# One more item for the last items' expert, and results finished in groups of four tiles

## The chip, the cores and the metric

One core of a Trainium2 chip runs one program. TensorE (PE) multiplies, VectorE (DVE) and ScalarE (ACT) work element by element, GpSimd (POOL) here issues indirect DMAs and computes powers, SyncE (SP) issues most of the other DMAs. The metric is the device time of one execution in microseconds (us).

## The reference

Two layers over 2048 tokens (2 sequences of 1024) of 512 numbers, all in float32. The first is a gated recurrence with a residual; the second a mixture of eight experts of which each token uses two.

```python
x = x + layernorm(minGRU(layernorm(x)))          # 512 -> 2*768 -> scan over 1024 -> 512
y = layernorm(x)
w, e = top_k(y @ gate_kernel, 2); w = softmax(w) # two experts of each token
out = sum over c of w[c] * (silu(y @ w0[e_c]) * (y @ w1[e_c])) @ wo[e_c]
x = x + layernorm(out)
```

An expert has two matrices of 512 x 1024 (w0, w1) and one of 1024 x 512 (wo), 2 MB each, 6 MB together.

## The kernel before, in words

**Blocks and tiles.** The 2048 tokens are four blocks of 512 tokens, a block is four tiles of 128. The recurrence goes block by block. As soon as a block's tokens are through it, they are routed: each of a token's two choices gets a row in a scratch list of its expert (`xs`), in the order of arrival, and POOL scatters the tokens there.

**Items.** The experts' work is cut into items: a run of up to 512 tokens of one expert. An item's tokens are read back from `xs` (four DMAs on SP, `fetch_tokens`), transposed by VectorE (`turn_in`), and multiplied in `run`: for each of 8 pieces of the hidden dimension, 4 matmuls with w0 and 4 with w1, silu on ScalarE, the product on VectorE, and 4 matmuls with wo. The columns of these matmuls are the item's tokens, rounded up to 8. The number of columns is known only at run time, so TensorE's program holds a copy (an arm) of the item for every size, and jumps to the right one (`Switch` in `emit`); `announce` hints at the next one. The result is transposed into `yo` and stored to `ys` by four DMAs, 256 KB each, issued when the next item's first matmul starts (`refill` calls `store`, `fetch_weights` for the next item, and `fetch_tokens` for a later one).

**Which items there are.** The first item runs while the last block is still being routed; it takes up to 512 tokens of the expert that has most in the first three blocks (`first_table`). The rest is planned from the counts on VectorE in `other_tables`. The expert with most tokens in the fourth block becomes the *last items' expert*: its tokens of tiles 12 to 14 are kept back for an item of their own (`last[0]`, slot `S_Z1` of `ys`), and tile 15 is computed for that expert as a dense tile straight from `late_y` (`last[1]`, `run_dense`). Everything else goes into `NR` = 14 regular items: every expert gets as many as its tokens need at 512 each, and the items that are left over are given one by one to the expert with most tokens per item (`most(length)`). An expert's tokens are spread evenly over its items, with sizes rounded up to 8. Regular items run in the order of experts. Weights lie in two buffers; an item's weights are loaded while the one before runs. The last item and the dense tile share one set.

**Finishing.** `places` works out for every token and choice in which row of `ys` its result stands. For each tile, two gathers (indirect DMAs on POOL) fetch the two results; ScalarE scales the first by its weight, VectorE adds the second, takes mean and variance, POOL raises the variance to the power -1/2, VectorE normalises and adds the residual, SP writes the tile out. Tiles 0 to 11 depend on the regular items alone; tiles 12 to 14 also on the last item's store. Tile 15 is gathered early without the last expert's part, and gets the dense tile's product at the very end (`finish_last`). Twelve pairs of buffers `got` hold the gathered rows; they lie on the weight buffer that the last items do not use. Tiles 12 to 15 use those of tiles 0 to 3 again.

**Order.** TensorE's order is the order of the recording. The other engines' orders come from a list scheduler (`schedule`) that simulates the program with the times written beside each operation (`ns`, `load`); `follows` adds an order without a wait, `urgent` puts an operation first. All orders are fixed when the kernel is built; an engine never overtakes within its own queue.

The lines that matter: the gathers come from `gather` (L1112 in the profile), the item's matmuls from `mm` in `run` (L1036), token transposes from `turn_in` (L999), DMAs from `dma` (L499); L303 is the recorder through which every other operation goes, so these are told apart by their tiles.

Of the kernel before, what the change touches and what calls it, by code (L numbers as in the profile page):

```python
# [319 lines left out]
def mingru_then_moe(nc, x, w_hg, w_out, w_gate, w0, w1, wo, out):  # L320
# [30 lines left out]

    B, S, D = x.shape
    DI = w_out.shape[0]
    E = w_gate.shape[1]
# [54 lines left out]
    minus_half, z_no, first_n, last_n, z1_n = (few[:, i : i + 1] for i in range(5))  # L411
    tw_late = few[:, 6:7]
    by = keep("by", [P, 4, E])
    first_e, total, z_one, count, start_e, so_far = (
# [6 lines left out]
    before_half = keep("before_half", [P, E])  # L421
    nums = {}
    for name, shape, pattern, base in (
        ("expert", [P, NT, E], [[0, NT], [1, E]], 0),
# [84 lines left out]


    g.POOL.memset(minus_half, -0.5)
    g.POOL.memset(ones, 1.0)
    g.POOL.affine_select(
        ident, ones, pattern=[[-1, P]], compare_op=ALU.is_equal, fill=0.0, base=0, channel_multiplier=1, ns=300
# [211 lines left out]
    def in_steps(n):  # L726
# [14 lines left out]

    def other_tables():

        pc = turn("tp", tp)[:, 0:E]
        g.PE.matmul(pc, ones, routed[NB - 1][1][:, NT - 1, :], start=True, stop=True, ns=280)
        g.DVE.tensor_copy(before_half, pc)
        pc = counts()
        g.DVE.tensor_copy(total, pc)
        new = little([P, E])
# [71 lines left out]
        z_row, z_at = little([P, E]), little([P, 1])  # L821
        g.DVE.tensor_add(z_row, before_half, first_row)
        g.DVE.tensor_mul(z_row, z_row, z_one)
        g.DVE.tensor_reduce(z_at, z_row, AX.X, ALU.add)
        g.DVE.tensor_copy(table_z[:, 1:2], z_at)
        g.DVE.tensor_copy(table_z[:, 0:1], z_no)
        z2, z2_n = little([P, E]), little([P, 1])
        g.DVE.tensor_sub(z2, total, before_half)
        g.DVE.tensor_mul(z2, z2, z_one)
        g.DVE.tensor_reduce(z2_n, z2, AX.X, ALU.add)  # L830
        g.DVE.tensor_sub(z1_n, last_n, z2_n)
        g.DVE.tensor_scalar(table_z[:, 3:4], in_steps(z1_n), -1.0, 0.0, ALU.add, ALU.max)

        g.DVE.tensor_scalar(by[:, 3, :], start, 2.0, float(W), ALU.add, ALU.mult)

    def places(c):
# [32 lines left out]
        g.DVE.tensor_scalar(z, z, z1_n, float((S_Z1 + 1) * W), ALU.subtract, ALU.add)  # L869

        late = slice(n - 1, n)
        early = little([P, 1])
# [36 lines left out]
    def fetch_tokens(it, behind=(), follows=()):  # L909

        j = it.no
        z = z_item[j % 2]
        if it is last[1]:
# [87 lines left out]
    def branch(its):  # L1001

        group = cells(its[0], 2)
        if len(its) > 1:
            group = table_i[0:1, 2, :]

        def load(e):
            for it in its:
# [15 lines left out]
    def run(it, gaps=()):  # L1024
# [8 lines left out]
        def mm(dst, w, rhs, first, last):  # L1033
            return g.add(
                "PE",
                lambda e, n: e.matmul(dst[:, W - n : W], w, rhs[:, W - n : W], start=first, stop=last),  # L1036
                [w, rhs] if first else [w, rhs, dst], [dst], 460 if most < W else 862, columns=1,
            )

        def down_part(m, q):  # L1040
# [4 lines left out]
        for m in range(KM):  # L1045
# [15 lines left out]
            if m == KM - 2 and it is not last[0]:  # L1061
                if it is first:
                    branch(regular)
                    branch(last[:1])
                announce(items[j + 1])
        yo = yo_item[j % 2]

# [11 lines left out]

    def run_dense(it):  # L1080

        g.item = last[0]
# [22 lines left out]
        return po[0]  # L1105


    def gather(dst, rows, slots, lane, i, follows=()):
        source = ys[0 : (slots[-1] + 1) * W, :]
        return g.add(  # L1110
            "POOL",
            lambda e: e.indirect_dma_start(dst, None, source, bass.IndirectOffsetOnAxis(ap=rows, axis=0)),  # L1112
            [rows] + [("ys", j, b) for j in slots for b in (*range(NQ), "nought")], [dst], 1450,
            lane=lane, batch=(i, lane), load=P * D * 4 / 320, follows=follows,
        )

    def finish(i):

        y0, y1 = got[0][i % NG], got[1][i % NG]
        for c, dst in ((0, y0), (1, y1)):  # L1120
            if i < TT - NT:
                o = gather(dst, where_i[:, c, i : i + 1], range(NR + 1), f"got{i % NG}", i)
            elif i < TT - 1:
                o = gather(dst, where_i[:, c, i : i + 1], range(S_Z1 + 1), f"got{i % NG}", i)
            else:
                o = gather(dst, where_early[:, c : c + 1], range(S_NONE + 1), f"got{i % NG}", i)
            gathers.append(o)
        g.ACT.activation(y0, y0, AF.Copy, scale=tw[:, 0, i : i + 1])
        g.DVE.scalar_tensor_tensor(y0, y1, tw[:, 1, i : i + 1], y0, ALU.mult, ALU.add)
        y0_v, y1_v, x_v = (  # L1130
            v.rearrange(how, c=NQ, b=NQ)
            for v, how in (
                (y0, "p (b c j) -> p b c j"), (y1, "p (c b j) -> p b c j"), (x_sb[i], "p (c b j) -> p b c j"),
            )
        )
        if i == TT - 1:
            g.DVE.tensor_copy(y1_v, y0_v)
            return y1
        mean, rstd = mean_and_rstd(y0)
        g.DVE.tensor_scalar(y0, y0, mean, rstd, ALU.subtract, ALU.mult)  # L1140
        g.DVE.tensor_add(y1_v, y0_v, x_v)
        dma("SP", of[ts(i, P), :], y1, f"out{i % NG}", P * D * 4, writes=[("out", i)])

    def finish_last(y, term):
        g.DVE.scalar_tensor_tensor(y, term, tw_late, y, ALU.mult, ALU.add)
# [15 lines left out]
    for t in range(NT - 1):  # L1161
# [18 lines left out]
    scan(  # L1180
        3, range(0, KE),
        gaps(
            [(turn_y, 2, 0), (turn_y, 2, 1)], [(rank, 1), (turn_y, 2, 2), (route, 2, 0, in_po)],
            [(turn_y, 2, 3), (route, 2, 1, in_po)], (route, 2, 2, in_po), (route, 2, 3, in_po), (),
            [(rank, 2), (first_table,)],
        ),
# [32 lines left out]
    drain(list(scattered.values()))  # L1219
    for it in items[1:-1]:  # L1220
        if it.no > 1:
            turn_in(items[it.no + 1], *((3, 4) if it is last[0] else ()))
        run(it)
    store(last[0])
    term = run_dense(last[1])
    gathers = []
    for i in (*range(TT - NT), TT - 1, *range(TT - NT, TT - 1)):
        if i == TT - 1:
            y = finish(i)
        else:  # L1230
            finish(i)
    drain(gathers)
    finish_last(y, term)

    g.emit()

# [41 lines left out]
```

## Time and profile before

| | us |
|---|---|
| runs | 998.93, 994.41, 998.54; median 998.54 |
| the profiled execution | 998.32 |
| its span (first to last instruction) | 996.3 |
| TensorE busy | 963.8 (97%) |
| VectorE, ScalarE, POOL busy | 434.8, 151.9, 110.4 |
| first regular item to the last item's end | 372.7 to 956.8 |
| the dense tile and all behind it | 956.8 to 996.3 |

The item sizes are the columns in the rows of L1036: the first item has 512, the regular ones, in the order of time, 256, 256, 256, 232, 232, 216, 136, 280, 288, 224, 216, 264, 264 and 128, the last item 272, the dense tile 128. Every matmul of float32 shows as two rows of TensorE, so an item has 192: 128 with w0 and w1, 64 with wo.

How to read what follows: in a list in order of time, the first two numbers are start and length in us, counted from the span's start; "x" is how many instructions were merged; the bracket is the engine's idle time before it and what ended it, where "issue" means that the profile shows nothing that was waited for. In a table of stretches each engine has its busy time and instruction count, followed by PEclk (the granted clock of TensorE, 1.00 is full speed), the mean busy share of the 16 DMA engines, and the GB/s moved.

### The profile page before, as it was taken

To read this page: it belongs to the slowest core of one execution; us is meant where nothing else is said; L and a number is where in the kernel's file an instruction comes from. 1 tells how busy PE (TensorE), PEld (TensorE's weight loads), DVE (VectorE), ACT (ScalarE), POOL (GpSimd) and SP (SyncE) were. 2 spreads that over 40 slices of the span, in tenths; PEclk is the share of its full clock that TensorE was granted. 3 is DMA by queue.
4 is the path that set the end of the run, shared out by engine and by line. 5 is a ranking of instruction groups with operands and counts; after the bars stand their busy time and mean duration, and the time that the engine had idled before them with its cause. 6 is when DMAs were issued, how large, how long until landed. Compare 5 with 4: busy or idle time off the path is not lost.

```text
span 996.3 us, 10882 instructions
## 1 busy us (share of the span) xinstructions
PE 963.8 (97%) x4086; PEld 713.8 (72%) x4086; DVE 434.8 (44%) x929; ACT 151.9 (15%) x269; POOL 110.4 (11%) x144
## 2 busy tenths in 40 slices
PE   6999999999999999999999999899999999998994
PEld 4444454555445448888899999787799988897882
DVE  6643636565465943313323324313224323142676
ACT  2222020212112001111011011110010110111221
POOL 3200104014312000000000000000000000000673
PEclk9999999999999999999999999999999999999997
DMA  9910002002821369596495696965475883836583
GB/s 298 388 64 1 0 1 86 0 1 95 273 108 64 126 192 320 163 279 231 110 324 171 183 316 190 325 188 208 132 258 159 262 289 66 293 129 214 151 256 130
DMA packets 140856, 175.40 MB, mean 176 GB/s; under 512 B 6112, under 2 KB 77792, under 8 KB 140768
## 3 DMA queue, kind: packets, MB, share of 16 engines
q1 hardware_dynamic: 132368, 155.22, 48.4%
q0 software_dynamic: 5120, 16.78, 5.1%
q10 hardware_dynamic: 3280, 2.10, 0.8%
q8 instruction: 70, 1.15, 0.5%
q14 instruction: 18, 0.15, 0.0%
HBM read 135.02 MB, written 39.06 MB: 175 GB/s over the span
## 4 chain that ended last, share of the span: by engine, by line
PE 91%; DMA 2%; POOL 2%; DVE 2%; issue 1%; ACT 0%; SPq 0%; DVEq 0%
PE bank L1036 63%; PE bank L303 28%; DMA got<-ys_scratch,where_i 2%; POOL got L1112 1%; DVE got L303 1%; POOL little L303 1%; DVE little L303 1%; DMA x<-in_L_attn_x_dram 0%; ACT got L303 0%; DVE inter L303 0%; DVE xn_in L303 0%; ACT xT L303 0%; ACT si L303 0%; SPq L1273 0%; DVEq L257 0%
## 5 line engine op out<-in xcount | busy, mean ns | idle before, releaser
L1036 PE MATMUL bank<-xTi,w 128*128 128x256 f32 (+10 forms) x2048 | 451.7, 379 | 8.0 <-issue 7.9
L1036 PEld LDWEIGHTS bank<-xTi,w 128*128 128x128 f32 x2048 | 369.3, 191 | 76.8 <-issue 37.3
L303 DVE TENSOR_TENSOR inter<-si,bank 128x512 f32<-128x512 f32 (+1 forms) x136 | 90.1, 662 | 371.1 <-PE bank L1036 370.8
L1036 PE MATMUL bank<-inter,wo 128*128 128x256 f32 (+10 forms) x1024 | 228.2, 376 | 0.0
L1036 PEld LDWEIGHTS bank<-inter,wo 128*128 128x128 f32 x1024 | 184.5, 190 | 33.9 <-issue 14.6
L303 PE MATMUL bank<-xT,whg 128*128 128x512 f32 (+1 forms) x400 | 171.5, 580 | 0.2 <-ACT xT L303 0.2
L303 ACT ACTIVATE si<-bank 128x512 f32<-128x512 f32 (+1 forms) x136 | 78.4, 577 | 557.3 <-PE bank L1036 555.7
L303 PEld LDWEIGHTS bank<-xT,whg 128*128 128x128 f32 x400 | 74.3, 192 | 77.5 <-issue 75.5
L1112 POOL DMA_INDIRECT got<-ys_scratch,where_i x30 | 31.1, 1036 | 602.2 <-DMA ys_scratch<-yo 594.7
L303 PE MATMUL bank<-wout,h 128*128 128x512 f32 x192 | 84.2, 595 | 0.0
L303 PEld LDWEIGHTS bank<-wout,h 128*128 128x128 f32 x192 | 35.9, 190 | 43.2 <-issue 41.1
L303 POOL TENSOR_TENSOR little<-little,few 128x1 f32<-128x1 f32 x64 | 40.3, 632 | 229.2 <-DVE little L303 228.9
L999 DVE STREAM_TRANSPOSE xTi<-zi 128x2048 f32<-128x2048 f32 (+2 forms) x18 | 63.3, 3514 | 4.5 <-DMA zi<-xs_scratch 4.5
L303 DVE STREAM_TRANSPOSE yo<-bank 128x512 f32<-128x512 f32 (+1 forms) x64 | 45.0, 702 | 37.1 <-PE bank L1036 33.7
L303 DVE SCALAR_TENSOR_TENSOR s<-bank,s 128x512 f32<-128x512 f32 x24 | 16.6, 690 | 78.8 <-ACT s L303 78.8
L704 POOL DMA_INDIRECT xs_scratch<-y,row_i x32 | 33.5, 1046 | 47.5 <-DVE little L303 33.7
L303 ACT ACTIVATE z<-bank 128x512 f32<-128x512 f32 x24 | 14.3, 597 | 109.5 <-PE bank L303 109.5
L303 DVE BATCH_NORM_STATS2 little<-x 128x6 f32<-128x512 f32 x32 | 21.7, 682 | 8.2 <-DMA x<-in_L_attn_x_dram 7.7
L303 ACT ACTIVATE s<-bank 128x512 f32<-128x512 f32 x24 | 14.3, 597 | 57.0 <-PE bank L303 57.0
L303 PEld LDWEIGHTS bank<-wg,yT 128*128 128x128 f32 x128 | 16.4, 192 | 5.3 <-issue 5.3
L303 PEld LDWEIGHTS bank<-ident,xn_in 128*128 128x128 f32 x64 | 8.6, 155 | 15.7 <-DVE little L303 8.7
L303 PE MATMUL bank<-ident,xn_in 128*128 128x128 f32 x64 | 11.2, 303 | 8.4 <-DVE little L303 8.3
(131 smaller groups left out, 366.7 us busy)
## 6 DMA issues: line engine op xcount, KB each, us to landing
w<-in_L_ffn_w_kernel_dram SPq DMA_DIRECT2D x64, 1024.0 KB, 9.0
wo<-in_L_ffn_wo_kernel_dram SPq DMA_DIRECT2D x32, 1024.0 KB, 14.0
zi<-xs_scratch SPq DMA_DIRECT2D x64, 256.0 KB, 5.5
ys_scratch<-yo SPq DMA_DIRECT2D x58, 256.0 KB, 10.1
xs_scratch<-nought SPq DMA_DIRECT2D x8, 1024.0 KB, 12.6
out_dram<-got SPq DMA_DIRECT2D x15, 256.0 KB, 3.0
x<-in_L_attn_x_dram SPq DMA_DIRECT2D x14, 256.0 KB, 7.8
whg<-in_L_attn_w_hg_dram SPq DMA_DIRECT2D x10, 256.0 KB, 6.7
```

Of the source, the lines that this page charges most:

```text
L303: return program.add(eng, lambda e: getattr(e, name)(*args, **kw), ins, [out], ns, urgent=urgent, follows=follows)
L704: lambda e, c=c, i=i: e.indirect_dma_start(xs, bass.IndirectOffsetOnAxis(ap=row_i[:, c, i : i + 1], axis=0), y_of[i], None),
L999: g.add("DVE", lambda e: e.transpose(dst, src), [z], [dst], 3900 // parts, follows=follows)
L1036: lambda e, n: e.matmul(dst[:, W - n : W], w, rhs[:, W - n : W], start=first, stop=last),
L1112: lambda e: e.indirect_dma_start(dst, None, source, bass.IndirectOffsetOnAxis(ap=rows, axis=0)),
```

## The change

Three things change.

*One more item.* The last items' expert gets an item for its tokens of the third block as well, as far as the first item did not take them (`z0_e`; `count_two` counts the tokens of blocks one and two for it). It has its own slot `S_Z0` in `ys`, can have any size up to 512, and runs between the regular items and the item of tiles 12 to 14. The regular items are planned for what is left; their number `NR` stays. Tiles 0 to 7 now wait for regular items alone, tiles 8 to 11 also for the new item's store.

*Groups.* The tiles are finished in groups of a block: all gathers of a group, then per tile the weighted sum and the statistics, then one power for the group's four variances (three in the last group), then normalising, residual and output tile by tile. A group's power is placed on POOL behind the gathers of the next group, and tile 15's two gathers come before the third group's power.

*Planner's times.* The scheduler's assumed times for gathers, for stores of the last items and for the new item's matmuls are changed.

```diff
-    NI = NR + 3
-    S_NONE, S_Z1 = NR + 1, NR + 2
+    NI = NR + 4
+    S_NONE, S_Z0, S_Z1 = NR + 1, NR + 2, NR + 3
...
+    def count_two():
+        pc = counts()
+        g.DVE.tensor_copy(before_two, pc)
...
+        g.DVE.tensor_max(z0_e, before_two, first_e)
+        g.DVE.tensor_sub(z0_e, so_far, z0_e)
...
-        g.DVE.tensor_scalar(z, one, last_n, None, ALU.mult)
+        g.DVE.scalar_tensor_tensor(z, z0_e, last_n, one, ALU.add, ALU.mult)
...
+        split = (NB - 1) * NT
+        g.DVE.tensor_scalar(z[:, 0:split], z[:, 0:split], z0_n, float((S_Z0 + 1) * W), ALU.subtract, ALU.add)
+        g.DVE.tensor_scalar(z[:, split:], z[:, split:], z0_n, z1_n, ALU.subtract, ALU.subtract)
+        g.DVE.tensor_scalar(z[:, split:], z[:, split:], float((S_Z1 + 1) * W), None, ALU.add)
...
-    last = [Item(NR + 1 + i, S_Z1, sizes[: LATE // STEP], (NR + 1) % 2) for i in range(2)]
+    last = [
+        Item(NR + 1 + i, slot, some, (NR + 1) % 2)
+        for i, (slot, some) in enumerate(((S_Z0, sizes), (S_Z1, sizes[: LATE // STEP]), (None, None)))
+    ]
...
-                load=most * P * 4 / (90 if it.no == NR else 320),
+                load=most * P * 4 / (160 if it.no >= NR else 320),
...
-                [w, rhs] if first else [w, rhs, dst], [dst], 460 if most < W else 862, columns=1,
+                [w, rhs] if first else [w, rhs, dst], [dst], 460 if it.no > NR else 862, columns=1,
...
-            [rows] + [("ys", j, b) for j in slots for b in (*range(NQ), "nought")], [dst], 1450,
-            lane=lane, batch=(i, lane), load=P * D * 4 / 320, follows=follows,
+            [rows] + [("ys", j, b) for j in slots for b in (*range(NQ), "nought")], [dst], 1270,
+            lane=lane, batch=(i, lane), load=1270,
...
+    def terms(i):
+
+        for c in range(2):
+            if i == TT - 1:
+                where, slots = where_early[:, c : c + 1], S_NONE
+            else:
+                where, slots = where_i[:, c, i : i + 1], (NR, NR, S_Z0, S_Z1)[i // NT]
+            o = gather(got[c][i % NG], where, range(slots + 1), f"got{i % NG}", i)
+        return o
...
+    def total_of(i):
         y0, y1 = got[0][i % NG], got[1][i % NG]
         g.ACT.activation(y0, y0, AF.Copy, scale=tw[:, 0, i : i + 1])
         g.DVE.scalar_tensor_tensor(y0, y1, tw[:, 1, i : i + 1], y0, ALU.mult, ALU.add)
...
+    def finish(tiles, behind):
+
+        n = len(tiles)
+        mv, rstd = little([P, n, 2]), little([P, n])
+        sums = [total_of(i) for i in tiles]
+        for k, (y0, _) in enumerate(sums):
+            st = little([P, 6])
+            g.DVE.bn_stats(st, y0)
+            g.DVE.bn_aggr(mv[:, k, :], st)
+        g.DVE.tensor_scalar(rstd, mv[:, :, 1], EPS, None, ALU.add)
+        g.POOL.tensor_tensor(rstd, rstd, minus_halves[:, 0:n], ALU.pow, ns=600, follows=behind)
+        for k, (i, (y0, y1)) in enumerate(zip(tiles, sums)):
+            g.DVE.tensor_scalar(y0, y0, mv[:, k, 0:1], rstd[:, k : k + 1], ALU.subtract, ALU.mult)
...
-    for i in (*range(TT - NT), TT - 1, *range(TT - NT, TT - 1)):
-        if i == TT - 1:
-            y = finish(i)
-        else:
-            finish(i)
+    groups = [range(n * NT, (n + 1) * NT - (n == NB - 1)) for n in range(NB)]
+    for tiles in groups[:-1]:
+        op = [terms(i) for i in tiles][-1]
+        if tiles[0]:
+            finish(prior, [op])
+        prior = tiles
+    op = terms(TT - 1)
+    y0, y1 = total_of(TT - 1)
...
+    finish(prior, [op])
+    op = [terms(i) for i in groups[-1]][-1]
+    finish(groups[-1], [op])
     drain(gathers)
-    finish_last(y, term)
+    finish_last(y1, term)
```

More of the change, by code (lines that the diff above doesn't have):

```diff
@@ L410, in mingru_then_moe @@
     few = keep("few", [P, 16])
-    minus_half, z_no, first_n, last_n, z1_n = (few[:, i : i + 1] for i in range(5))
+    minus_halves = few[:, 12:16]
+    minus_half, z_no, first_n, last_n, z0_n, z1_n = (few[:, i : i + 1] for i in range(6))
     tw_late = few[:, 6:7]
@@ L420, in mingru_then_moe @@
     where_early = table_e[:, 8:10]
-    before_half = keep("before_half", [P, E])
+    before_last, before_two, z0_e = (keep(n, [P, E]) for n in ("before_last", "before_two", "z0_e"))
     nums = {}
@@ L511, in mingru_then_moe @@
     g.POOL.memset(minus_half, -0.5)
+    g.POOL.memset(minus_halves, -0.5)
     g.POOL.memset(ones, 1.0)
@@ L745, in other_tables @@
         g.PE.matmul(pc, ones, routed[NB - 1][1][:, NT - 1, :], start=True, stop=True, ns=280)
-        g.DVE.tensor_copy(before_half, pc)
+        g.DVE.tensor_copy(before_last, pc)
         pc = counts()
@@ L819, in other_tables @@
         g.DVE.tensor_scalar(table_i[:, 2, :], n_steps, -1.0, 0.0, ALU.add, ALU.max)
[L821 to L825, printed above, removed]
-        g.DVE.tensor_copy(table_z[:, 0:1], z_no)
[L827 to L832, printed above, removed]
+        for i, until in enumerate((so_far, before_last)):
+            z_row, z_at = little([P, E]), little([P, 1])
+            g.DVE.tensor_add(z_row, until, first_row)
+            g.DVE.tensor_mul(z_row, z_row, z_one)
+            g.DVE.tensor_reduce(z_at, z_row, AX.X, ALU.add)
+            g.DVE.tensor_copy(table_z[:, 1 + i : 2 + i], z_at)
+        g.DVE.tensor_copy(table_z[:, 0:1], z_no)
+        of_z = little([P, 2, E])
+        g.DVE.tensor_mul(of_z[:, 0, :], z0_e, z_one)
+        g.DVE.tensor_reduce(z0_n, of_z[:, 0, :], AX.X, ALU.add)
+        g.DVE.tensor_sub(of_z[:, 1, :], before_last, so_far)
+        g.DVE.tensor_mul(of_z[:, 1, :], of_z[:, 1, :], z_one)
+        g.DVE.tensor_reduce(z1_n, of_z[:, 1, :], AX.X, ALU.add)
+        for i, n in enumerate((z0_n, z1_n)):
+            g.DVE.tensor_scalar(table_z[:, 3 + i : 4 + i], in_steps(n), -1.0, 0.0, ALU.add, ALU.max)
         g.DVE.tensor_scalar(by[:, 3, :], start, 2.0, float(W), ALU.add, ALU.mult)
@@ L868, in places @@
         g.DVE.tensor_scalar(is_z, z, 0.0, None, ALU.is_ge)
-        g.DVE.tensor_scalar(z, z, z1_n, float((S_Z1 + 1) * W), ALU.subtract, ALU.add)
+        split = (NB - 1) * NT
+        g.DVE.tensor_scalar(z[:, 0:split], z[:, 0:split], z0_n, float((S_Z0 + 1) * W), ALU.subtract, ALU.add)
+        g.DVE.tensor_scalar(z[:, split:], z[:, split:], z0_n, z1_n, ALU.subtract, ALU.subtract)
+        g.DVE.tensor_scalar(z[:, split:], z[:, split:], float((S_Z1 + 1) * W), None, ALU.add)
         late = slice(n - 1, n)
@@ L912, in fetch_tokens @@
         z = z_item[j % 2]
-        if it is last[1]:
+        if it is last[2]:
             return [
@@ L1004, in branch @@
         if len(its) > 1:
-            group = table_i[0:1, 2, :]
+            group = table_z[0:1, 3:5] if its[0] is last[0] else table_i[0:1, 2, :]
         def load(e):
@@ L1060, in run @@
                     down_part(m - LAG, q)
-            if m == KM - 2 and it is not last[0]:
+            if m == KM - 2 and it is not last[1]:
                 if it is first:
                     branch(regular)
-                    branch(last[:1])
+                    branch(last[:2])
                 announce(items[j + 1])
@@ L1080, in run_dense @@
     def run_dense(it):
-        g.item = last[0]
+        g.item = last[1]
         a, b, c = weights[it.weights]
@@ L1105, in run_dense, with gather @@
         return po[0]
-    def gather(dst, rows, slots, lane, i, follows=()):
+    def gather(dst, rows, slots, lane, i):
         source = ys[0 : (slots[-1] + 1) * W, :]
-        return g.add(
+        o = g.add(
             "POOL",
             lambda e: e.indirect_dma_start(dst, None, source, bass.IndirectOffsetOnAxis(ap=rows, axis=0)),
-            [rows] + [("ys", j, b) for j in slots for b in (*range(NQ), "nought")], [dst], 1450,
-            lane=lane, batch=(i, lane), load=P * D * 4 / 320, follows=follows,
-        )
@@ L1117, in finish @@
-    def finish(i):
-        y0, y1 = got[0][i % NG], got[1][i % NG]
[L1120 to L1124, printed above, removed]
-            else:
-                o = gather(dst, where_early[:, c : c + 1], range(S_NONE + 1), f"got{i % NG}", i)
-            gathers.append(o)
+            [rows] + [("ys", j, b) for j in slots for b in (*range(NQ), "nought")], [dst], 1270,
@@ new lines, in gather @@
+            lane=lane, batch=(i, lane), load=1270,
+        )
+        gathers.append(o)
+        return o
+    gathers = []
+    def terms(i):
[5 more added lines that the diff above has]
+            o = gather(got[c][i % NG], where, range(slots + 1), f"got{i % NG}", i)
+        return o
+    def total_of(i):
+        y0, y1 = got[0][i % NG], got[1][i % NG]
@@ L1128, in finish @@
         g.ACT.activation(y0, y0, AF.Copy, scale=tw[:, 0, i : i + 1])
         g.DVE.scalar_tensor_tensor(y0, y1, tw[:, 1, i : i + 1], y0, ALU.mult, ALU.add)
[L1130 to L1133, printed above, removed]
-            )
-        )
-        if i == TT - 1:
-            g.DVE.tensor_copy(y1_v, y0_v)
-            return y1
-        mean, rstd = mean_and_rstd(y0)
@@ L1140, in finish @@
-        g.DVE.tensor_scalar(y0, y0, mean, rstd, ALU.subtract, ALU.mult)
-        g.DVE.tensor_add(y1_v, y0_v, x_v)
-        dma("SP", of[ts(i, P), :], y1, f"out{i % NG}", P * D * 4, writes=[("out", i)])
+        return y0, y1
+    def finish(tiles, behind):
[10 more added lines that the diff above has]
+            g.DVE.tensor_scalar(y0, y0, mv[:, k, 0:1], rstd[:, k : k + 1], ALU.subtract, ALU.mult)
+            g.DVE.tensor_add(
+                y1.rearrange("p (c b j) -> p b c j", c=NQ, b=NQ), y0.rearrange("p (b c j) -> p b c j", c=NQ, b=NQ),
+                x_sb[i].rearrange("p (c b j) -> p b c j", c=NQ, b=NQ),
+            )
+            dma("SP", of[ts(i, P), :], y1, f"out{i % NG}", P * D * 4, writes=[("out", i)])
@@ L1182, in mingru_then_moe @@
         gaps(
-            [(turn_y, 2, 0), (turn_y, 2, 1)], [(rank, 1), (turn_y, 2, 2), (route, 2, 0, in_po)],
+            [(turn_y, 2, 0), (turn_y, 2, 1)], [(rank, 1), (count_two,), (turn_y, 2, 2), (route, 2, 0, in_po)],
             [(turn_y, 2, 3), (route, 2, 1, in_po)], (route, 2, 2, in_po), (route, 2, 3, in_po), (),
@@ L1221, in mingru_then_moe @@
         if it.no > 1:
-            turn_in(items[it.no + 1], *((3, 4) if it is last[0] else ()))
+            turn_in(items[it.no + 1], *((3, 4) if it is last[1] else ()))
         run(it)
-    store(last[0])
-    term = run_dense(last[1])
-    gathers = []
-    for i in (*range(TT - NT), TT - 1, *range(TT - NT, TT - 1)):
-        if i == TT - 1:
-            y = finish(i)
-        else:
-            finish(i)
+    store(last[1])
+    term = run_dense(last[2])
+    groups = [range(n * NT, (n + 1) * NT - (n == NB - 1)) for n in range(NB)]
[6 more added lines that the diff above has]
+    y0, y1 = total_of(TT - 1)
+    g.DVE.tensor_copy(
+        y1.rearrange("p (c b j) -> p b c j", c=NQ, b=NQ), y0.rearrange("p (b c j) -> p b c j", c=NQ, b=NQ)
+    )
+    finish(prior, [op])
+    op = [terms(i) for i in groups[-1]][-1]
+    finish(groups[-1], [op])
     drain(gathers)
-    finish_last(y, term)
+    finish_last(y1, term)
     g.emit()
```

## The prediction

> **What bounds the kernel now.** I read the page's chain that ended last first, then TensorE alone in order of time, then the busy time of each stretch, then the last 80 us in order of time.
>
> ```profile
> q8 instruction: 70, 1.15, 0.5%
> ...
> PE 91%; DMA 2%; POOL 2%; DVE 2%; issue 1%; ACT 0%; SPq 0%; DVEq 0%
> ```
>
> The last line says that the span is a TensorE story with a short tail of gathers and finishing; the first, that instructions themselves come by DMA, in pieces of 1.15 MB / 70 = 16 KB. So what counts is TensorE's time up to the last item, and the tail behind it.
>
> ```profile
> 609.00 9.52 PE L1036 MATMUL bank<-xTi,w 128*128 128x136 f32 x80 [0.37 <-issue]
> 634.48 20.77 PE L1036 MATMUL bank<-xTi,w 128*128 128x280 f32 x80 [2.99 <-issue]
> 800.39 18.06 PE L1036 MATMUL bank<-xTi,w 128*128 128x264 f32 x80 [0.59 <-issue]
> 911.16 20.14 PE L1036 MATMUL bank<-xTi,w 128*128 128x272 f32 x80 [3.63 <-issue]
> ```
>
> Each row opens an item; the bracket is the idle time before it. TensorE stops 2.99 us behind the item of 136 columns and 3.63 us behind the one of 128, but 0.37 and 0.59 us behind those of 216, and not at all behind 264, 280 or 288. The releaser is "issue": no data and no engine was waited for. The shorter the item, the longer the stop when its successor's code is jumped to.
>
> ```profile
> core 0: us, PE busy (x), PEclk, DMA share, GB/s
> 609.00:634.48 25.48, 22.49 (x192) 1.00 0.94 312
> 681.51:728.07 46.56, 46.56 (x194) 1.00 0.56 182
> 764.50:800.39 35.89, 35.30 (x193) 1.00 0.73 236
> 800.39:843.21 42.82, 42.82 (x193) 1.00 0.62 198
> 843.21:885.93 42.72, 42.72 (x194) 1.00 0.52 180
> 885.93:911.16 25.23, 21.60 (x194) 1.00 0.84 294
> 911.16:956.80 45.64, 45.64 (x192) 0.97 0.55 152
> 956.80:996.30 39.50, 23.78 (x145) 0.83 0.59 191
> ```
>
> One item a row, start to start: 136, 288, 216, 264, 264, 128 columns, the last item of 272, then the dense tile with everything behind it. Time is nearly proportional to columns: (35.30 - 22.49) / 80 = 0.160 us a column. Splitting an item costs almost no matmul time.
>
> ```profile
> 631.50:634.40 2.90, 0.00 (x0) 0.00 (x0) 2.58 (x5) 0.00 (x0) 0.00 (x0) 1.00 0.86 201
> 634.40:637.90 3.50, 3.42 (x8) 2.54 (x9) 0.44 (x1) 0.00 (x0) 0.00 (x0) 0.51 0.99 188
> 800.00:803.50 3.50, 3.11 (x14) 2.70 (x15) 0.91 (x2) 0.60 (x1) 0.00 (x0) 1.00 0.23 43
> ```
>
> The column before the DMA share is the granted clock. Behind the stop of 2.99 us it is 0.51 for 3.5 us; behind that of 0.59 us it stays 1.00. The lost half is about 1.7 us, which the item of 272 shows too: at 0.160 a column it should take 46.56 - 16 x 0.160 = 44.0 us and takes 45.64.
>
> **The change, part by part: which items there are.** Counting the reference's choices for these inputs gives 762, 679, 134, 277, 281, 438, 1399 and 126 tokens for experts 0 to 7; expert 6 is both the first item's and the last items' expert, with 371, 323 and 362 tokens in blocks two, three and four. Fed to the planner's rules, these counts give exactly the sizes in the rows above, so I trust the same arithmetic for the new rules. The new item takes the 323 tokens of block three: 328 columns. Expert 6 is left with 202 tokens, one regular item of 208 instead of two of 264. That frees one of the 14 regular items, and the rule hands it to the expert with the most tokens per item, expert 4: its 288 becomes 144 and 144. Columns over all items rise by 8; the last item stays at 272.
>
> **TensorE up to the last item.** The 288 goes (46.56), two of 144 come, each 22.49 + 8 x 0.160 = 23.8: +1.0. Two of 264 go (85.54), one of 208 comes, 35.30 - 1.28 = 34.0: -51.5. Each 144 is followed by a jump that its own length must hide. By the line from 136 (2.99) to 216 (mean 0.48) the stop is 2.7; bounds 2.4 (going on from 128 through 136) and 3.0. Twice 2.7: +5.4. The 208 leaves a stop of 0.7 before the 128, where there was none: +0.7. The clock behind the two new stops: bounds 0 (the 0.59 us row) and 1.7 each (the 2.99 us row); 2.7 is nearest to 2.99, so 1.7 each: +3.4. Sum -41.0. The new item: 46.56 + 40 x 0.160 = 52.9, plus the 1.7 of clock behind the 128's stop, which it now pays in the last item's place: +54.6, and the last item -1.7. One more counting matmul in the third scan, 0.3. TensorE reaches the dense tile 12.2 us later, at 969.0.
>
> [...]
>
> Weights and tokens: the new item shares the last item's weights, so 14 regular loads stay 14. Every load starts with its predecessor; the 25.48 us of the 136 carried a full one at DMA share 0.94, and the 144s last 23.8 + 2.7 = 26.5. Nothing is late there; were it so, each further us would fall on TensorE twice. The new item adds four token loads on SP behind the stores of a regular item and four stores, two on SP and two on ACT, at its own end; SP's results for tiles 0 to 3 stand before these and are due some 35 us into the new item, 20 us ahead.
>
> The planner's extra work on VectorE is about a dozen small instructions of 0.15 to 0.2 us, 2 us, before the first regular item's weights are asked for at 337.7; that item starts at 372.7. Half of those 35 us cover the loads; without cover it would cost the 2 us.
>
> **The tail.** Behind the dense tile's start it is now 39.5 us. Its rows:
>
> ```profile
> 919.57 0.98 POOL L1112 DMA_INDIRECT got<-ys_scratch,where_i  x1 [594.68 <-DMA ys_scratch<-yo]
> ...
> 959.59 1.13 ACTq L499 DMA_DIRECT2D ys_scratch<-yo  x2
> 979.14 0.95 POOL L1112 DMA_INDIRECT got<-ys_scratch,where_i  x1 [0.30 <-issue]
> 982.81 0.72 ACT L303 ACTIVATE got<-got,tw 128x512 f32<-128x512 f32 x1 [1.11 <-DMA got<-ys_scratch,where_i]
> 990.76 0.75 DVE L303 SCALAR_TENSOR_TENSOR got<-got,little,x 128x512 f32<-128x512 f32 x1 [0.51 <-POOL little L303]
> ```
>
> POOL starts 8.4 us into the last item (911.16 to 919.57) and strings 30 gathers of about 1.27 us, and a power for every tile, up to 980.7: its queue, not the last store, sets the last gather. After the change the sixteen gathers of tiles 0 to 7 start 8.4 us into the new item and take 20 us; those of tiles 8 to 11 start 8.4 us into the last item and take 10, with 25 us to spare. So the fewer powers save nothing on the path of these tiles: their cover is the two items. Only the last three tiles stand behind the last store. From the dense tile's start: transposes of 384 columns done at 1.1; issue 1.1 and landing 6.1 (a 192 KB store's time on ACT), 8.3; five more gathers at 1.27, then 3.7 to land (979.14 to 982.81), 18.4; ACT 0.72 and VectorE's weighted sum 0.75, 19.9; the dense tile's product queued behind, 0.28; statistics 0.69, 0.17, 0.15, and the power 0.6 to 1.0, 22.1; three normalisations of 0.53, three additions of 0.69 and a product of 0.28, overlapping a little, 25.5; the last tile's own sum, statistics, power and final step 3.2, 28.7; from there to the end as now, 991.5 to 996.3, 4.8. That is 33.5, so -6.0. Bounds 32 (store and landing at their fastest) and 39.5 (nothing gained). The new wait is in grouping: no tile of a group is normalised until the group's last statistics are there. Behind the waiting power stand gathers that are not yet due; on VectorE the dense tile's last two products stand behind it, which is in the sum.
>
> Span 996.3 + 12.2 - 6.0 = 1002.5; the profiled run took 998.32 in all, 2.0 more than its span, so 1004.5. The median of the runs shown, 998.54, is 0.2 from that run; the forecast lies 0.6% over it.
>
> **Rivals.** *The stops come, the clock holds:* 3.4 less, 1001.1. For it: both halved stretches follow stops longer than 2.7. Against it: 2.99 sufficed.
> *The 144s do not stop (other side):* the 136 ran with DMA share 0.94, and its successor's code pages may have queued behind weights; the 144s may meet a freer moment. Then 5.4 + 3.4 + 0.7 go, 995.0. It decides once the stops and clocks at the 144s cost under 2.6 together. Against it: the 128's stop was the longest, with a DMA share of 0.19 while it lasted. With a tail at 32 it ends at 993.5, half a per cent faster.
> *ScalarE blocks:* in the dense tile now ScalarE stood 5.2 us in its queue for a gather with the matmuls' silu behind it. In the new order the silus of the new, the last and the dense item stand behind gathers' scalings; if those land late the tail keeps its 39.5: 1010.5. Against it: each scaling has some 5 us of a wider item between its gather and the next silu.
> *The sizes come out differently:* a token or two of rounding moves a column step, 1.3 us; inside the range.
>
> **How the numbers follow.** Forecast 0.45, clock holds 0.25, no stops 0.17, ScalarE 0.13. About 0.5%, 5 us, is what a measurement of this kernel can tell from no change; the three runs of before spread over 4.5 us. Slower by more: the forecast but for a few runs of luck, and ScalarE, together 0.57. Within: clock holds, and half of no stops: 0.31. Faster: the rest, 0.12. The forecast's own range is 1002 to 1008 (tail and stop bounds); taking in the clock case and some of the others it is 997 to 1009.
>
> **What would show it.** Right: rows of 328, 208 and two of 144 columns; 2.4 to 3.0 us of "issue" behind each 144 with clock 0.5; the dense tile about 12 us later; POOL idle before the last six gathers; some 33 us from the dense tile's start to the end. Wrong: no stop behind a 144, a clock of 1.00 there, or a wait of TensorE for ScalarE inside the new item.

## The result, and the profile after

| | before | changed |
|---|---|---|
| median of 21 runs each | 997.76 us | 1001.77 us |
| lowest to highest | 994.41 to 1000.83 | 997.73 to 1004.34 |
| ratio, 95% interval | | 1.0035 [1.0025, 1.0045] |
| span of the profiled run | 996.3 us | 996.0 us |
| dense tile starts, in the profile | 956.8 | 963.5 |
| from there to the end | 39.5 | 32.5 |

The change makes the kernel slower by 0.35%, 3.5 to 4 us. The profiled run of the changed kernel was the fastest of its 21 runs (997.73), so its span hides the loss; what it shows must be read together with the profiles of the experiments.

First TensorE in order of time, the rows that open an item (start, length, idle time before it in brackets), of the changed kernel:

```profile
634.04 19.12 PE L1056 MATMUL bank<-xTi,w 128*128 128x280 f32 x80 [2.81 <-issue]
679.41 9.96 PE L1056 MATMUL bank<-xTi,w 128*128 128x144 f32 x80
704.88 10.06 PE L1056 MATMUL bank<-xTi,w 128*128 128x144 f32 x80 [1.78 <-issue]
732.04 16.87 PE L1056 MATMUL bank<-xTi,w 128*128 128x224 f32 x80 [3.38 <-issue]
805.57 14.32 PE L1056 MATMUL bank<-xTi,w 128*128 128x208 f32 x80 [0.19 <-issue]
864.76 24.01 PE L1056 MATMUL bank<-xTi,w 128*128 128x328 f32 x80 [3.14 <-issue]
```

There are the two items of 144 columns in place of one of 288, the 208 in place of two of 264, and the new item of 328. Four stops of TensorE are longer than 1 us where before had two; the two new ones stand behind the 144s. Then the busy time of one item a row, start to start: the two 144s, the 224 behind them, the 128, the new item, the last item, and the dense tile with all behind it (TensorE's busy time, granted clock, DMA share, GB/s):

```profile
core 0: us, PE busy (x), PEclk, DMA share, GB/s
679.41:704.88 25.47, 23.69 (x193) 1.00 0.95 322
704.88:732.04 27.16, 23.78 (x193) 0.99 1.01 319
732.04:770.09 38.05, 38.05 (x192) 0.96 0.69 223
839.92:864.76 24.84, 21.70 (x193) 1.00 0.87 306
864.76:919.50 54.74, 54.74 (x193) 0.97 0.44 127
919.50:963.50 44.00, 44.00 (x194) 1.00 0.40 120
963.50:996.00 32.50, 21.59 (x145) 0.87 0.37 106
```

Two 144s take 52.6 us where the 288 took 46.6. The 224 behind them takes 38.05 where it took 36.43, at a clock of 0.96. The last row is the gain: 32.5 for 39.5. POOL, in order of time, shows where it comes from:

```profile
873.26 0.99 POOL L1132 DMA_INDIRECT got<-ys_scratch,where_i  x1 [548.61 <-DMA ys_scratch<-yo]
927.62 0.96 POOL L1132 DMA_INDIRECT got<-ys_scratch,where_i  x1 [18.73 <-DMA ys_scratch<-yo]
946.85 1.01 POOL L303 TENSOR_TENSOR little<-little,few 128x4 f32<-128x4 f32 x1 [8.38 <-DVE little L303]
970.24 1.01 POOL L1132 DMA_INDIRECT got<-ys_scratch,where_i  x1 [22.38 <-DMA ys_scratch<-yo]
976.57 0.95 POOL L1132 DMA_INDIRECT got<-ys_scratch,where_i  x1 [0.30 <-issue]
```

Each group's gathers now wait for a store (8.5 us into the new item, 8.1 into the last, 6.7 into the dense tile), and POOL stands idle for 22 us before the last six. Its queue no longer sets when the last six begin.

### The profile page after: what moved, and what is told of

Same layout as the page of the kernel before. It is cut to its first block, busy times and chain, and to the rows that moved or that the text cites. A ratio compares the mean times of both kernels' runs of the same rounds, so it can differ in the third digit from the quotient of the medians.

```text
span 996.0 us, 11340 instructions
## 1 busy us (share of the span) xinstructions
PE 964.2 (97%) x4280; PEld 721.3 (72%) x4280; DVE 448.8 (45%) x946; ACT 156.8 (16%) x277; POOL 100.1 (10%) x134
## 4 chain that ended last, share of the span: by engine, by line
PE 94%; issue 2%; DVE 1%; DMA 1%; POOL 1%; ACT 0%; POOLq 0%; ACTq 0%; SPq 0%; DVEq 0%
PE bank L1056 66%; PE bank L303 28%; DVE little L303 1%; DVE got L303 0%; DMA ys_scratch<-yo 0%; POOL got L1132 0%; DMA x<-in_L_attn_x_dram 0%; DMA got<-ys_scratch,where_i 0%; POOL little L303 0%; DVE xn_in L303 0%; POOLq L1238 0%; DVE yo L303 0%; ACT xT L303 0%; ACT got L303 0%; DVE inter L303 0%
## 5 line engine op out<-in xcount | busy, mean ns | idle before, releaser
L1056 PE MATMUL bank<-xTi,w 128*128 128x256 f32 (+11 forms) x2176 | 453.8, 366 | 12.2 <-issue 12.1
L1056 PEld LDWEIGHTS bank<-xTi,w 128*128 128x128 f32 x2176 | 374.9, 191 | 78.0 <-issue 44.1
L303 DVE TENSOR_TENSOR inter<-si,bank 128x512 f32<-128x512 f32 (+1 forms) x144 | 95.7, 665 | 356.3 <-PE bank L1056 348.2
L1056 PE MATMUL bank<-inter,wo 128*128 128x256 f32 (+11 forms) x1088 | 229.5, 364 | 0.0
L1056 PEld LDWEIGHTS bank<-inter,wo 128*128 128x128 f32 x1088 | 187.7, 190 | 31.9 <-issue 14.8
L303 ACT ACTIVATE si<-bank 128x512 f32<-128x512 f32 (+1 forms) x144 | 83.3, 579 | 567.2 <-PE bank L1056 549.0
L1132 POOL DMA_INDIRECT got<-ys_scratch,where_i x30 | 29.1, 972 | 597.9 <-DMA ys_scratch<-yo 589.7
L1019 DVE STREAM_TRANSPOSE xTi<-zi 128x2048 f32<-128x2048 f32 (+2 forms) x19 | 67.2, 3537 | 4.2 <-DMA zi<-xs_scratch 4.2
L303 DVE STREAM_TRANSPOSE yo<-bank 128x512 f32<-128x512 f32 (+1 forms) x68 | 47.8, 703 | 40.4 <-PE bank L1056 36.4
L303 POOL TENSOR_TENSOR little<-little,few 128x1 f32<-128x1 f32 (+2 forms) x53 | 32.9, 624 | 229.7 <-DVE little L303 229.6
L303 DVE BATCH_NORM_STATS2 little<-x 128x6 f32<-128x512 f32 x32 | 21.7, 682 | 7.8 <-DMA x<-in_L_attn_x_dram 7.2
L303 PEld LDWEIGHTS bank<-ident,xn_in 128*128 128x128 f32 x64 | 8.7, 155 | 15.3 <-DVE xn_in L303 8.3
```

Source lines behind the costliest of these rows:

```text
L303: return program.add(eng, lambda e: getattr(e, name)(*args, **kw), ins, [out], ns, urgent=urgent, follows=follows)
L1019: g.add("DVE", lambda e: e.transpose(dst, src), [z], [dst], 3900 // parts, follows=follows)
```

## The experiments

Ratios are against the kernel before, in runs on the same chip; its medians there were 999.22 (first four), 997.82 (the next three), 998.05 (four) and 998.71 us (the last).

| kernel | median us | ratio, 95% interval |
|---|---|---|
| grouping alone | 995.33 | 0.9964 [0.9952, 0.9976] |
| new item alone | 1001.53 | 1.0022 [1.0007, 1.0036] |
| changed, 13 regular items | 993.07 | 0.9938 [0.9924, 0.9953] |
| before, 15 regular items | 1007.81 | 1.0093 [1.0069, 1.0116] |
| changed, hint in third piece | 1060.45 | 1.0620 [1.0592, 1.0649] |
| changed, spare item elsewhere | 1000.01 | 1.0022 [1.0010, 1.0034] |
| changed, less weight traffic | 991.67 | 0.9942 [0.9928, 0.9957] |
| changed, hint in sixth piece | 1064.41 | 1.0595 [1.0570, 1.0620] |
| changed, hint in fifth piece | 1059.98 | 1.0619 [1.0581, 1.0657] |
| grouping alone, hint in sixth | 1046.41 | 1.0487 [1.0463, 1.0512] |
| 13 regular items, hint in sixth | 1049.41 | 1.0515 [1.0484, 1.0546] |
| before, 13 regular items | 994.77 | 0.9963 [0.9949, 0.9978] |

### The two halves of the change, each alone

The planner's times, the third part of the change, have no run of their own: those for the gathers go with the grouping in the first kernel, and all of them stay in the second.

**Grouping alone.** The kernel before with the changed kernel's `gather`, `terms`, `total_of`, `finish` and final loop; tiles 0 to 11 wait for the regular items.

```diff
-                where, slots = where_i[:, c, i : i + 1], (NR, NR, S_Z0, S_Z1)[i // NT]
+                where, slots = where_i[:, c, i : i + 1], (NR, NR, NR, S_Z1)[i // NT]
```

> The kernel before with the grouped finishing alone: no new item, tiles 0 to 11 still wait for regular items only. Theory (the 7 us shorter tail comes from POOL's queue: with few powers in it, the last six gathers wait for the last store alone): POOL starts about 8.4 us into the last item, 24 gathers of 1.27 us and tile 15's two are through some 34 us later, before the last store lands; the dense tile's start stays, and what follows it shrinks from 39.5 to 33 to 35 us, so 5 to 6.5 us faster than before, ratio 0.994 to 0.995. Rival (the tail is shorter because the new item moves twelve tiles' finishing to an earlier time): without the item VectorE has four tiles to finish beside the dense tile, the tail stays within 2 us of 39.5, ratio 0.998 to 1.000.

Faster by 0.36% (0.24 to 0.48), less than the theory's 0.5 to 0.6 and more than the rival's 0 to 0.2. The dense tile started at 956.51 and the rest took 36.1 us. POOL in order of time:

```profile
964.23 0.96 POOL L1114 DMA_INDIRECT got<-ys_scratch,where_i  x1 [6.83 <-DMA ys_scratch<-yo]
968.96 1.04 POOL L303 TENSOR_TENSOR little<-little,few 128x4 f32<-128x4 f32 x1
971.76 1.71 POOL L1114 DMA_INDIRECT got<-ys_scratch,where_i  x1 [0.31 <-issue]
```

As the theory has it, POOL was ahead of the last store and the first of the last six gathers waits for that store, not for the queue. But tiles 8 to 11 are still being finished beside the dense tile, as the rival has it: their power cuts into the six gathers, and the last of these starts 15.3 us behind the dense tile's start where the changed kernel needs 13.1. Each account is worth about half: the tail is 3.4 us shorter than before, where the whole change makes it 7.0 shorter.

**New item alone.** The changed kernel with each tile finished by itself, one power a tile, in the order of before.

```diff
-    groups = [range(n * NT, (n + 1) * NT - (n == NB - 1)) for n in range(NB)]
...
+    for i in (*range(TT - NT), TT - 1, *range(TT - NT, TT - 1)):
+        if i == TT - 1:
+            y = finish(i)
+        else:
+            finish(i)
```

> The changed kernel, but with every tile finished by itself and a power of its own, as before. Theory: with the new item POOL has tens of us to spare, so powers in its queue cost nothing and the time is that of the changed kernel within 2 us, ratio to before 1.002 to 1.006; what follows the dense tile's start is 32 to 34.5 us. Rival (grouping is what shortens the tail): the tail goes back towards 39.5, ratio 1.008 to 1.011.

1.0022 beside the 1.0035 of the whole change, with intervals that overlap: with the new item the grouping is worth nothing that these runs can tell. The row of the dense tile and all behind it, in the busy times by stretch, is as short as in the changed kernel:

```profile
970.89:1002.10 31.21, 21.59 (x145) 0.91 0.39 111
```

So the tail is shortened by finishing twelve tiles beside earlier items. Grouping is another way to about half of the same gain; the two don't add.

### The price of the two items of 144 columns

**13 regular items** in the changed kernel (enough for these inputs, not for all), so that 288 stays whole:

```diff
-    NR = (2 * T - LEAST_A - LEAST_Z + E * (W - 1)) // W
+    NR = (2 * T - LEAST_A - LEAST_Z + E * (W - 1)) // W - 1
...
-    got = [[g.sbuf(f"got{c}_{i}", [P, D], base + (2 * i + c) * 2 * K) for i in range(NG)] for c in range(2)]
+    got = [[g.sbuf(f"got{c}_{i}", [P, D], base + 48 * K + (2 * i + c) * 2 * K) for i in range(NG)] for c in range(2)]
```

> The changed kernel with 13 regular items in place of 14 (enough for these inputs), so that expert 4's 288 columns stay whole; the buffers of the gathered rows move to the other weight buffer, which is then the free one. Theory (the two items of 144 cost stops of TensorE and the halved clock behind them): against the changed kernel the two items with their stops, 52.6 us, become 46.6, and the clock loss of up to 1.7 behind the second goes: 6 to 8 us faster than the changed kernel, 2 to 4 us faster than before, ratio 0.996 to 0.998. Rival (the loss is the new item's own, in its loads, stores and the wider program): the ratio stays at 1.002 to 1.004.

**15 regular items** in the kernel before (the same edit with + 1; the gathered rows move to the other buffer here too), which splits the 288 and leaves the other items as they are:

> The kernel before with 15 regular items in place of 14 and nothing else of the change: the rule gives the additional item to expert 4, 288 becomes 144 and 144. Theory: 1.0 us of columns, two stops of 1.8 to 3.4 us behind the 144s, and 0 to 1.7 us of clock behind each: 5 to 9 us slower, ratio 1.005 to 1.009, all of it ahead of the last item. Rival (splitting is free): ratio 1.000 to 1.002.

The first is 0.97% below the changed kernel (0.9938 to 1.0035), 9.7 us, and 6 us faster than before; the second is 9.3 us slower than before (6.9 to 11.6). Against the new item alone, which has the same items and ran on the same chip, the first is 8.5 us faster. Taken away from the one or added to the other, the pair of 144s is worth some 8 to 10 us, more than the first theory's 6 to 8 and about the upper end of the second's 5 to 9. Both rivals fall. The profiles give the same size: from the start of the first 144 to the start of the item behind the 224 TensorE needs 90.7 us in the changed kernel, 93.7 with the new item alone and 91.3 with 15 items, where the 288 and its 224 took 83.0 before. In the second, TensorE's rows behind the 144s are

```profile
707.63 10.06 PE L1036 MATMUL bank<-xTi,w 128*128 128x144 f32 x80 [2.30 <-issue]
734.54 16.85 PE L1036 MATMUL bank<-xTi,w 128*128 128x224 f32 x80 [3.13 <-issue]
```

and in the first, the new item, the last item and the tail, by stretch:

```profile
860.48:915.22 54.74, 54.74 (x192) 0.97 0.44 127
915.22:959.22 44.00, 44.00 (x193) 1.00 0.40 120
959.22:991.60 32.38, 21.59 (x145) 0.88 0.37 106
```

Here the dense tile starts 2.4 us later than before (959.2 to 956.8) and the tail is 7.1 shorter: that is the new item without its side effect. Of the versions that do all of the work this is the fastest that ran, faster than both kernels. Of those that serve inputs in general it is the grouping alone, which leaves the number of items as it was.

**Any item, or only one that leaves a stop?** Two more kernels move the boundary elsewhere. One gives the spare item to the expert whose items would still be largest with one more:

```diff
-            g.DVE.tensor_scalar(parts, count, 1.0, None, ALU.max)
+            g.DVE.tensor_scalar(parts, count, 1.0, None, ALU.add)
```

> The changed kernel with one operation of the planner changed: an item that is left over goes to the expert whose items would still be largest with one more (tokens over count + 1), not to the one whose items are largest now. 14 regular items as before the edit, but the spare one goes to expert 0: 192, 192, 192, 192 in place of 256, 256, 256, and expert 4 keeps its 288. Theory: a 192 leaves a stop of 0.2 to 0.9 us and no loss of clock, so against the changed kernel 52.6 + 1.6 us of the 144s become 46.6, and three or four stops of 0.2 to 0.9 us come: 4 to 7 us faster than the changed kernel, 0 to 3 us faster than before, ratio 0.997 to 1.000. Rival (an added regular item costs the same wherever it is put, by its loads, its store and its jump): ratio 1.002 to 1.005.

The ratio, 1.0022 (1.0010 to 1.0034), is the rival's, and my theory missed: the 192s were not cheap. Against the changed kernel with 13 items, which has neither the 192s nor the 144s, they cost 0.84%, 8.4 us. TensorE's rows behind the four 192s:

```profile
407.85 16.23 PE L1056 MATMUL bank<-xTi,w 128*128 128x192 f32 x80 [2.77 <-issue]
443.28 13.26 PE L1056 MATMUL bank<-xTi,w 128*128 128x192 f32 x80 [0.99 <-issue]
475.33 13.26 PE L1056 MATMUL bank<-xTi,w 128*128 128x192 f32 x80 [0.59 <-issue]
507.65 15.92 PE L1056 MATMUL bank<-xTi,w 128*128 128x232 f32 x80 [0.86 <-issue]
```

The first stop is as long as one behind a 144, and its successor's first 80 matmuls take 16.2 us for 13.2: 3 us of clock. The stop's length is not the item's length alone. What differs in the profile is the DMA engines' share: 1.02 through the first 192, 0.82 to 0.96 through the other three, and next to nothing (0.03 and less) while the four stops lasted. Whether that is why the first stop is the long one is not shown here. The other kernel is before with 13 regular items (the edit shown above), where expert 1's 232, 232 and 216 become 344 and 336:

> The kernel before with 13 regular items in place of 14 (enough for these inputs); the gathered rows move to the other weight buffer. Expert 1's 232, 232, 216 become 344 and 336, and no short item is touched. Theory (an item costs by the stop that it leaves, and 232 and 216 leave 0 to 0.4 us): one boundary and its stop less, 0.5 to 2 us faster than before, ratio 0.998 to 1.000. Rival (any item costs some 8 us, as the 144s, the 192s and the 15th item did, by its loads, its store and its jump): ratio 0.991 to 0.993.

0.9963, 3.7 us (2.2 to 5.1): below the rival's 7 to 9, above the theory's 0.5 to 2. In its profile the two items take 109.8 us for the 111.7 of the three, and the clock held behind the 128, 1.5 us; what makes the rest of the median is open. So one item more between long ones costs about 2 us in the rows and 3.7 in the median, and one that makes 144s or 192s costs 8 to 10.

### What the stop is made of

**Less weight traffic.** The changed kernel without the loads of wo from the third item on.

```diff
-        for half in range(2):
+        for half in range(0 if j > 1 else 2):
```

> The changed kernel without the loads of wo from the third item on: every item's second product uses the wo that the first two items left in the buffers, so a third of each item's weight bytes is gone; sizes and instructions stay. Theory (the stop is set by the item's own length): the stops behind 136, 144, 144 and 128 stay within 0.5 us of 2.8, 1.8 to 2.8, 3.0 to 3.4 and 3.1, ratio 1.000 to 1.005. Rival (the code's pages wait behind weights on the DMA engines): the stops in which the DMA engines are busy, those behind 136 and the 144s, lose 1 to 2 us each and their clock loss, ratio 0.990 to 0.997.

TensorE behind 136, 144, 144 and 128 columns:

```profile
633.54 19.13 PE L1056 MATMUL bank<-xTi,w 128*128 128x280 f32 x80 [1.68 <-issue]
704.42 10.06 PE L1056 MATMUL bank<-xTi,w 128*128 128x144 f32 x80 [1.82 <-issue]
729.51 15.39 PE L1056 MATMUL bank<-xTi,w 128*128 128x224 f32 x80 [1.31 <-issue]
859.88 22.33 PE L1056 MATMUL bank<-xTi,w 128*128 128x328 f32 x80 [1.65 <-issue]
```

The four stops come to 6.5 us where the changed kernel had 2.81, 1.78, 3.38 and 3.14, 11.1; the first 80 matmuls behind them run at full speed; and the kernel is 0.93% faster than the changed one. My theory, length alone, falls: a third of the weight bytes is worth about 1.2 us a stop on average, (11.1 - 6.5) / 4, and the clock loss that it brings on. It is not the same for each: three stops lose 1.1, 2.1 and 1.5 us, the one of 1.78 loses nothing. The stop behind the 128, which the rival had left out, loses 1.5. While these stops last the DMA engines stand at 0.00, where the changed kernel has 1.10, 1.10, 0.97 and 0.33; through the short items themselves they still run at 0.78 to 0.88. The 1.6 us that remain on average may be the item's length and whatever the other two thirds add; the runs don't part these. The edit also spares SP the issue of these loads, 4.20 us (at 709.05) and 4.36 us (at 736.14) for two of the items in the changed kernel's profile, so that the order of the transfers may have a share in it. The kernel multiplies by a stale wo, so this is an experiment and no version to use.

**The hint.** Three kernels give the hint at the next item earlier than in the seventh of eight pieces; two more combine the sixth piece with the faster versions.

```diff
-            if m == KM - 2 and it is not last[1]:
+            if m == (KM - 2 if it is first else 5) and it is not last[1]:
```

> The changed kernel with the hint at the next item (announce) in the third of the eight pieces of every item instead of the seventh; sizes, items and orders stay. Theory A (the stop is the time from the hint to the next item's code, and a short item leaves too little of it): the stops behind 136, 144, 144 and 128 columns fall under 0.6 us and the clock stays at 1.00, 10 to 14 us faster than the changed kernel, ratio to before 0.989 to 0.994. [...] Rival C (an early hint's pages are pushed out again by the item's own code): every item stops some us, ratio over 1.02.

> The changed kernel with the hint one piece earlier, in the sixth of eight pieces (the third had cost 3 us behind long items and 6 behind short ones). Theory (the hint's pages come late behind a short item, and survive as long as the item's own code has all been fetched by then): one piece of a 144 is 2.9 us, so the stops behind 136, 144, 144 and 128 fall by 1.5 to 2.9 us each and the clock is no longer halved there: 8 to 13 us faster than the changed kernel, ratio to before 0.991 to 0.996. Rival (the item's own later pages push the hinted ones out from here on as well): stops of 3 us behind most items, ratio over 1.03.

> The same with the hint in the fifth piece. [...] Rival (the fifth piece is as good as the sixth): within 0.3% of that run.

> The kernel before with the grouped finishing alone and the hint in the sixth piece. Theory: the 3.9 us of the grouping (ratio 0.9964) and the two stops behind 136 and 128 with their clock, 3 to 8 us: ratio 0.988 to 0.993. Rival (the hint does not help): 0.996 to 0.997.

> The changed kernel with 13 regular items and the hint in the sixth piece. Theory: the ratio of 0.994 that 13 items gave and the same two stops, 3 to 8 us: 0.986 to 0.991. Rival: 0.993 to 0.995.

With the third piece the ratio of rival C, over 1.02, came true (1.0620); why every item stopped was not shown, and that the sixth piece would be better than the seventh was my guess. It was as bad, and so was the fifth (1.0619, for a forecast of 1.00 to 1.04): 5 to 6% slower in all five, so that my theories for all of them missed; for the last two even the rivals, which had the hint do nothing. TensorE with the hint in the sixth piece, behind 256, 256, 136 and 144 columns:

```profile
416.69 17.52 PE L1056 MATMUL bank<-xTi,w 128*128 128x256 f32 x80 [2.54 <-issue]
461.32 19.21 PE L1056 MATMUL bank<-xTi,w 128*128 128x256 f32 x80 [2.93 <-issue]
667.25 20.88 PE L1056 MATMUL bank<-xTi,w 128*128 128x280 f32 x80 [6.54 <-issue]
747.53 12.60 PE L1056 MATMUL bank<-xTi,w 128*128 128x144 f32 x80 [6.87 <-issue]
```

Over the five profiles the stops are 1.8 to 3.9 us behind items of 208 to 328 columns and 4.4 to 6.9 behind those of 128 to 144. They still depend on the item's length; no run shows the reason. Why the sixth piece is already too early was not shown either; each kernel moves as many instruction packets as the same kernel with the hint in the seventh piece (74, and 70 in the last two), so the count does not tell them apart. A hint later than the seventh piece wasn't tried.

## Why the prediction was right, and where it was off

The measured 1001.77 lies in the range, 997 to 1009, and 2.7 us under the forecast of 1004.5. The loss was forecast as 0.6% and is 0.35%, so the case that came true is "within 0.5%", to which I had given 0.31 (its own terms, 0.25 and half of 0.17, add up to 0.335). The measured time lies just under the 1002 to 1008 that I gave for the forecast alone, and next to the rival in which the clock holds, 1001.1. The baseline is part of it: I counted from 998.54, the median of three runs, and the median of 21 is 997.76.

**Sizes and columns: right.** The items are the forecast ones. The busy times are 23.7 and 23.8 for the 144s (forecast 23.8), 34.0 for the 208 (34.0), 54.7 for the new item with its clock loss (54.6), 44.0 for the last (43.9).

**The pair of 144s: right in sum, wrong in its reason.** Forecast 1.0 + 5.4 + 3.4 = 9.8 us; measured 9.7 (taken away) and 9.3 (added). In three profiles the stops behind the 144s were 1.78 and 3.38, 2.80 and 3.01 (new item alone), 2.30 and 3.13 (15 items): 2.73 on average for my 2.7. That the average fits so well is partly luck: the single stops lie outside my bounds of 2.4 and 3.0 on both sides. And I took the length of the item as the cause and put the traffic of weights among the rivals, as all or nothing; a third less of it takes two fifths of four such stops away, and an item of 192 columns left a stop of 2.77.

**The clock: less than forecast.** I took 1.7 us behind each of the two. Of the six stops behind 144s in these three profiles four were followed by a halved clock. In the changed kernel's own profile the stop of 2.81 us was not, where 2.99 us had been before. The three stretches of 3.5 us behind its stops of 2.81, 1.78 and 3.38 us, with the clock ahead of the DMA share:

```profile
634.04:637.54 3.50, 3.50 (x15) 1.00 0.74 168
704.88:708.38 3.50, 3.50 (x28) 1.00 0.76 193
732.04:735.54 3.50, 3.50 (x11) 0.57 0.28 65
```

The forecast had the dense tile at 969.0, it started at 963.5, and 3.4 of the 5.5 us are two halvings that did not happen; most of the rest is stops that were shorter, 1.9 us in sum. In the profile of the new item alone all four came and the dense tile started at 970.9; behind its 144s the first 80 matmuls took 11.7 and 17.1 us, for 10.1 and 15.3 at full clock:

```profile
708.16 11.73 PE L1056 MATMUL bank<-xTi,w 128*128 128x144 f32 x80 [2.80 <-issue]
736.62 17.07 PE L1056 MATMUL bank<-xTi,w 128*128 128x224 f32 x80 [3.01 <-issue]
```

This goes far to explain why the profiled run is 4 us under the median of its kind: over the 21 runs time and mean granted clock go together (correlation -0.82; 0.987 in the two slowest, 0.992 in this one). The length of the stop alone does not settle it: the clock was halved behind stops of 2.80 and 3.01 us (new item alone), and not behind one of 2.81 (changed kernel, 1.00 over the 3.5 us behind it) or one of 3.60 (before with 13 items).

**The tail: a mis-sized term.** Forecast 33.5 us from the dense tile's start, -6.0; measured 32.5 in the changed kernel, 32.4 with 13 items and 31.2 with the new item alone, so -7 to -8. The term that was off is the last store: I added 1.1 of issue and 6.1 of landing, but the landing counts from the issue. The stores went out at 964.54, 1.0 behind the dense tile's start, and the first gather started at 970.24, 5.7 us later: 6.7 in all for my 8.3. From there every step came 1.4 to 1.7 us before its forecast time, and the way from the last instruction to the end was 0.4 longer.

**What was to cost nothing** did: with the new item a power for every tile changes nothing that the runs can tell (1.0022 beside 1.0035), and TensorE waits for no ScalarE inside an item: in the changed kernel's profile all its waits from 372.7 to 963.5 are "issue", 12.1 us in 8 stops. But "the fewer powers save nothing" holds only beside the new item; in the kernel before, the whole grouping, fewer powers and a new order together, is worth 3.9 us.

**The rivals.** The clock held behind two of the six stops, about 1.1 of the 3.4 us by an estimate from these three profiles. The 144s did stop, against the second; that weight traffic lengthens a stop has support nonetheless from the run with less of it, 6.5 us for 11.1 over four stops. ScalarE did not block: none of TensorE's 12.1 us of waits from the first regular item to the dense tile is put down to it.

Put together from measured terms: +2.4 (dense tile's start with 13 items) + 9.5 (the pair) - 7.1 (tail) = 4.8 us, beside the measured 3.5 to 4.0. The first and the last are from one profile each, and the 9.5 rests in part on the changed kernel's own time, so the sum only shows that the terms agree.

## What to carry to other kernels

Count what a planner does with the slack that a change leaves: the new item paid about 6 us, and the regular item that it freed was spent on cutting another expert's work in two, which cost 8 to 10. In these runs the jump to the next item's code cost more behind short items (2.99 us behind 136 columns and 3.63 behind 128, 0.37 and 0.59 behind 216, in the kernel before), and less when there was less weight traffic (6.5 us for 11.1 over four stops), so short items were dear even though their matmul time was nearly proportional to columns (21.7 us for 128, 23.7 for 144, 34.0 for 208, 54.7 for 328 with its clock loss). When two edits shorten the same tail, try each alone first: here either is enough for much of the gain.

## What the hardware did that I had not expected

- The stops were longer beside weight traffic: with a third of the weight bytes gone, four of them fell from 11.1 to 6.5 us in sum, in one profile of each kernel, and none was followed by a halved clock.
- A hint in the sixth piece or earlier did harm: in the five profiles every boundary stopped, 1.8 to 3.9 us behind items of 208 columns and more and 4.4 to 6.9 behind those of 128 to 144, 5 to 6% of the kernel.
- Whether a stop near 3 us cost another 1.7 us of clock (up to 3.1 behind some) changed from run to run, and this goes with a good part of the changed kernel's scatter; what decides it in a run is not shown. Over the 14 profiles of this study, counting stops of TensorE of 1 us and more ahead of an item behind the first regular one: under 2.1 us none of 8 was followed by a halved clock, from 2.1 to 2.7 us 2 of 12, from 2.7 to 3.3 us 27 of 44, above that 32 of 36.
